# Small results in two halves of one PSUM bank, identity transposes spread over set-up and the last two sequences, and a new table of the order

## The chip, the core and the metric

The kernel runs on one core of a Trainium2 chip. Its time is the device time of one execution in microseconds (us). Each core has five engines that run their own instruction streams and meet by semaphores: PE (TensorE, matrix products), DVE (VectorE), ACT (ScalarE), POOL (GpSimd) and SP (SyncE, which here issues the DMAs). PE writes its results to PSUM, 8 banks of 128 partitions x 512 float32; DVE and ACT read them there. All other tiles are in SBUF.

## The reference

32 sequences of 256 tokens x 256 features, float32, go through two attention layers, each followed by a conditioned output block. What is computed, for one sequence:

```python
# layer 0: linear attention, 8 heads of 32
xn = ln(x, ln_w, ln_b)
q = softmax((xn @ Wq + bq) by head, over the 32 features)
k = softmax((xn @ Wk + bk + (1 - mask) * -1e6) by head, over the tokens)
v = (xn @ Wv + bv) * mask
y = q @ (k^T v)                       # per head
x = x + block(y, emb, ...)
# layer 1: full attention, 16 heads of 16
xn = ln(x, norm_w, norm_b)
q, k, v = xn @ q_w + q_b, xn @ k_w + k_b, (xn @ v_w + v_b) * mask
a = softmax(q k^T + (1 - mask) * -1e6)   # the mask goes by the key
y = a v
out = x + block(y, emb, ...)
# block
scale, shift = split(silu(emb) @ W_emb + b_emb)
block = silu(ln(y) * (1 + scale) + shift) @ W_out + b_out
```

Products are float32 in precision: each operand is split into a high and a low part, and three products of parts are added.

## The kernel before

Each sequence is cut into some 150 steps, each a small function that issues instructions on one engine: `scores` on PE, `maxima` on DVE, `exp` on ACT, and so on. Four parts of a sequence have letters that end the step's name in the tables: a is the input of layer 0 (load, normalisation, q, k, v, softmaxes, attention), b is the output block of layer 0, c is the input of layer 1 with its scores and weighted values, d is the output block of layer 1. Set-up (`prepared`) is a graph of the same kind: loads of the weights, folding of the norms into them (`w_sums`, `w_scaled`, `w_high`, `w_low`), the modulation (`e_product`, `e_sums`, `e_scaled`), the memsets of the score operands (`qk_zeros`, L510, two memsets of 128x2048 each, three times), and `identity`, `identity_r` (L269 to L275).

The order is written out in a table. STARTS gives each step of a sequence a planned start; sequence b's is PERIOD = 26.2851 later than that of b − 1. SHIFTS moves the parts a to d of the first three and last five sequences. SET_UP does the same for set-up. `in_order` (L113) sorts all steps by planned start and issues them in that order; a step whose tiles are not free waits in a list until they are. ROOM says how many tiles of each kind there are: 8 banks, for instance. Since one list decides, each engine's program order is fixed when the kernel is built, about five sequences being under way at once. On the chip, an engine runs its own list in order and stops where a semaphore is not yet there. These semaphores are put in by the framework from what each instruction reads and writes; in PSUM two engines are kept apart by the whole bank.

Layer 1 goes twice over the scores. First `scores` (L1029; two banks of 128x512) and `maxima` (L1041, DVE) find the maximum of each row. `max_high`, `max_low` (POOL) split it, `max_turn` (L1061, PE) turns it into rows, `max_row` (L1068, ACT) copies them out of PSUM, and a DMA (`max_place`) puts them into the operand of the second pass. There `scores` come again (L1096), `exp` (L1108, ACT), and `pv` (L1117, PE) weights the values: two for each half c of the features, v = 0 and 1, into one bank. `y_blocks` (L1136, DVE) transposes that bank, `y_sums` and `y_over` divide by the sums. `v_masked` (L1011, ACT) writes the operand va of pv, of which there are two buffers: it waits for the pv of two sequences before.

The output block of layer 1 (`normalized_blocks`, L621) takes statistics on DVE (`stats`, L625), adds them over partitions by a small product on PE (`means`, L630), goes on through `mean`, `spread` (DVE), `squared` (ACT), `added` (DVE), `variances` (PE, same bank), `variance` (DVE) to `deviation` (POOL), and then on to the gate and the product with W_out (`productd`, L558 like all split products). In layer 0, `attention` (L883, PE) writes a bank that `k_sums` and `blocks` (DVE) read.

The steps that the change touches took one of the 8 banks each: `means` with `variances`, `attention`, `max_turn`, and `pv` (one for v = 0 and 1). `warmed` (L277) is 16 transposes of the identity at the start of set-up, whose result nobody reads.

"Quick" sequences (the first EARLY = 2 and the last FINAL = 1) have some of POOL's work on DVE.

Of the kernel before, what the change touches and what calls it, by code (L numbers as in the profile page):

```python
# [10 lines left out]
F32 = mybir.dt.float32  # L11
# [12 lines left out]
    bank=8, xt=9, nrm=4, x=4, h=2, g=6, k0=3, ek=1, mk=1, q0=1, y=2, eqT=2, v0=2, att=1, qkp=1, qk=3,  # L24
# [7 lines left out]
NWARM = 16  # L32
# [4 lines left out]
    addedd=(120.61,), attentiona=(-13.38,), baseb=(-7.73,), based=(88.15,), blocksa=(-11.52,),  # L37
    centredd=(121.30,), deviationa=(-83.15,), deviationb=(-6.20,), deviationc=(24.49,), deviationd=(124.48,),
    dividedd=(125.42,), expc=(89.70, 92.11, 89.98, 91.28, 96.74, 97.83, 98.71, 99.15, 94.09, 94.56, 96.29,
    94.59, 101.15, 101.17, 101.20, 101.90), gateb=(-0.05,), gated=(129.02,), gatedb=(3.48,), gatedd=(133.75,),  # L40
    higha=(-72.32,), highc=(26.27,), k_expa=(-26.36,), k_kepta=(-19.92,), k_maxa=(-28.80,),
    k_producta=(-31.27,), k_sumsa=(-11.80,), k_turna=(-22.62,), loada=(-239.80,), lowa=(-51.26,), lowc=(29.93,),
    mask_rowa=(-53.49,), mask_rowsc=(33.40,), max_highc=(79.75,), max_lowc=(79.77,), max_placec=(88.54,),
    max_rowc=(82.68,), max_turnc=(82.00,), maximac=(55.40, 55.77, 56.53, 60.59, 56.43, 58.64, 64.05, 63.87,
    57.93, 60.08, 71.94, 73.05, 77.62, 78.88, 78.57, 77.29), meand=(116.76,), meansd=(116.59,),
    offseta=(-80.64,), offsetb=(-3.77,), offsetc=(24.78,), productb=(16.97,), productd=(142.80,), pvc=(92.35,
    100.35, 97.30, 103.38), q_expa=(-33.30,), q_lessa=(-33.32,), q_maxa=(-36.69,), q_producta=(-40.25,),
    q_turna=(-37.20,), q_turneda=(-11.84,), qk_highc=(33.74, 36.00), qk_lowc=(34.71, 41.81), qk_productc=(31.72,
    34.63), qk_wholec=(33.95, 40.07), resultb=(19.28,), resultd=(143.38,), scaleda=(-78.72,), scaledb=(-2.75,),
    scaledc=(25.24,), scoresc=(53.73, 56.51, 56.39, 60.97, 57.39, 70.48, 76.30, 75.27, 88.56, 89.96, 95.03,  # L50
    96.09, 92.06, 93.94, 99.31, 99.65), split_highb=(4.18,), split_highd=(135.42,), split_lowb=(13.04,),
    split_lowd=(138.42,), spreadd=(117.00,), squaredd=(119.35,), stack_lowc=(45.83,), stackc=(37.76,),
    statsa=(-103.45,), statsb=(-7.70,), statsc=(23.10,), statsd=(114.46,), stored=(150.83,), turna=(-73.69,),
    turnb=(-1.20,), turnc=(25.77,), turnedd=(128.51,), v_maskedc=(54.65,), v_productc=(51.60,),
    values_producta=(-24.01,), valuesa=(-22.73,), varianced=(122.21,), variancesd=(121.52,), wholea=(-72.30,),
    wholec=(28.29,), y_blocksd=(102.83, 105.24), y_overa=(-9.70, -8.79), y_overd=(104.23, 112.01),
    y_producta=(-10.85,), y_sumsa=(-9.72, -8.93), y_sumsd=(104.21, 108.21),
# [3 lines left out]
    0: (0.0, 0.0, 0.0, 0.0), 1: (0.0, 0.0, 0.0, 0.0), 2: (0.0, 0.0, 0.0, 0.0), 27: (0.0, 0.0, 0.0, 0.0),  # L61
    28: (0.0, 0.0, 0.0, 0.0), 29: (0.0, 0.0, 0.0, 0.0), 30: (0.0, 0.0, 0.0, 0.0), 31: (0.0, 0.0, 0.0, 0.0),
# [3 lines left out]
    bias_scaled=(-248.02,), cond_silu=(-161.41,), cond_tanh=(-332.90,), diag_made=(-816.08,), e_out=(-48.80,  # L66
    -2.85), e_product=(-96.24, -2.87), e_scaled=(-22.24, -1.46), e_sums=(-48.78, -2.83), identity=(-708.56,),
    identity_r=(-702.04,), load_bias=(-276.37,), load_bout=(-13.79, 53.66), load_cols=(-670.58,),
    load_cond=(-544.29,), load_emb=(-258.80, -217.52, -180.67, -207.44, -42.77, -14.95, -48.76, -2.89),
    load_masks=(-359.47,), load_w=(-291.77, -528.39, -390.22, -548.16, -39.72, -33.64, -88.51, -232.84),  # L70
    mask_terms=(-103.15,), p_made=(91.90, 5.63), qk_made=(-52.44, 60.07, 77.11), qk_zeros=(-61.21, -379.66,
    -674.55), qkp_made=(30.64,), terms0_store=(-141.84,), terms_rows=(-172.06,), terms_store=(-42.73,),
    terms_turn=(-333.70,), token_terms=(-574.41,), v0_made=(-369.51, -279.71), va_made=(-36.90, 52.97),
    w_high=(-50.10, -64.76, -198.98, -439.51, 25.73, 18.32, 14.13, -231.47), w_low=(-39.74, -58.97, -95.39,
    -307.80, 29.41, 24.14, 30.22, 4.56), w_rep=(-292.96, -366.10), w_scaled=(-76.66, -94.61, -210.46, 20.45,
    9.77, -47.81), w_sums=(-179.39, -114.53, -238.08, 19.55, 7.28, -54.52), warmed=(-409.56,),
    zero_one=(-762.96,), zero_one_store=(-98.07,),
# [87 lines left out]
def tile_two_layers(ctx: ExitStack, tc: tile.TileContext, a: dict, out: bass.AP):  # L165
# [34 lines left out]

    def f(ap):
        return ap.bitcast(F32)
# [49 lines left out]

    def prepared():
# [23 lines left out]
        def warmed():  # L277
            ps = bank()
            for n in range(NWARM):
                nc.tensor.transpose(ps[:, ts(n % 4, P)], ident, ident)  # L280

        o_cols = op("D", 0.3, load_cols)
        o = op("G", 0.9, identity)
        op("P", 0.11 * NWARM, warmed, o, take=("bank",), give=("bank",))
# [291 lines left out]
    def sequence(b):  # L576
# [44 lines left out]
        def normalized_blocks(*after):  # L621
# [8 lines left out]
            def means():  # L630
                s.m_sum = bank()
                nc.tensor.matmul(s.m_sum[:, 0:16], fold4, s.st[:, :, 1:6:3], start=True, stop=True)
# [21 lines left out]
            def variance():  # L654
                s.var = small.tile([P, NBLOCK], F32, name="var", bufs=4)
                nc.vector.tensor_reduce(s.var, s.m_sum[:, 16:32].rearrange("p (g n) -> p g n", n=2), AX.X, ALU.add)

# [21 lines left out]
            o = op("P", 0.15, means, o_s, take=("bank",))  # L679
# [5 lines left out]
            o = op("V", 0.12, variance, o, give=("bank",))  # L685
# [197 lines left out]
        def attention():  # L883
            s.a_ps = bank()[:, 0 : NC * 33].rearrange("p (c l) -> p c l", c=NC)
# [13 lines left out]
        def blocks():  # L898
            s.att = work.tile([P, NC, 4, 33], F32, name="att", bufs=ROOM["att"])
            for c in range(NC):  # L900
                nc.vector.scalar_tensor_tensor(
                    s.att[:, c], s.a_ps[:, c].unsqueeze(1).to_broadcast([P, 4, 33]), s.rk[:, c : c + 1], diag,
                    ALU.mult, ALU.mult,
                )

        o = op("P", 0.29, attention, o_k, o_v, take=("bank",), give=("k0", "v0"), mode=2)
        o = op("V", 0.12, k_sums, o)
        o_a = op("V", 0.42, blocks, o, done["diag"], take=("att",), give=("bank",))
# [152 lines left out]
        def max_turn():  # L1061
            s.m_ps = bank(F32R)
# [5 lines left out]
        def max_row():  # L1068
            s.m_row = work.tile([4 * NU * NC, S], F32R, name="m_row", bufs=ROOM["mrow"])
            nc.scalar.copy(s.m_row, f(s.m_ps[0 : 4 * NU * NC, 0:S]))  # L1070

# [5 lines left out]
        o = op("P", 0.13, max_turn, o, take=("bank",), give=("mx",))  # L1077
        o = op("A", 0.27, max_row, o, take=("mrow",), give=("bank",))
# [3 lines left out]
        s.yT_ps, s.yT = [None] * NC, [None] * NC  # L1082
# [5 lines left out]
        for c in range(NC):  # L1088
            o_pv = []
            for v in range(2):  # L1090
# [26 lines left out]
                def pv(c=c, v=v):  # L1117
                    if v == 0:
                        s.yT_ps[c] = bank()
# [118 lines left out]
```

## Time and profile before

| what | us |
|---|---|
| median of three runs (917.66, 918.82, 920.21) | 918.82 |
| the profiled execution | 914.85 |
| its span, from the first to the last instruction | 912.7 |
| PE busy | 864.9 |
| DVE busy | 813.5 |
| ACT busy | 700.2 |
| POOL busy | 692.4 |

The span is what the engines' records cover; 2.2 us of the execution lie around it. The profiled execution is 4.0 us under the median of the others. In the slices of the page each digit stands for 22.8 us: PE is at 9 tenths from the sixth to the thirty-eighth slice with no gap, lower in the head (6, 8, 7, 8, 8) and in the tail (7, 3). The line PEclk is the clock that was granted to PE: 6 and 7 tenths in the first two slices, 8 and 5 in the last two.

Of the groups, the longest on DVE are the maxima of the scores (324.9 us), on ACT the exponentials (270.2 us), on PE the split products of L558 (seven forms of some 80 to 150 us each).

### The profile page before, as it was taken

The page shows a single profiled execution, that of the slowest core. Times are in us where ns is not written, and L with a number is a line of the kernel's source. Part 1 is how long each engine was busy: PE and PEld are TensorE (multiplying, and loading weights), DVE is VectorE, ACT ScalarE, POOL GpSimd, SP SyncE. Part 2 cuts the span into 40 slices and gives each one's busy share as a digit, 9 for nine tenths or more (in the row PEclk, how much of TensorE's full clock was granted, in tenths as well). Part 3 has the DMA queues.
Part 4 walks back from the last instruction along what each step waited for, and adds up shares of the span by engine and source line. Part 5 has one row for each costly group of instructions (what it writes and reads, how often), then busy time and mean ns, then how long its engine had stood idle before and what let it go on. Part 6 is the DMA issues. An engine that isn't in the chain of part 4 may idle for free.

```text
span 912.7 us, 25210 instructions
## 1 busy us (share of the span) xinstructions
PE 864.9 (95%) x9494; PEld 705.0 (77%) x9494; DVE 813.5 (89%) x2235; ACT 700.2 (77%) x1420; POOL 692.4 (76%) x893
## 2 busy tenths in 40 slices
PE   6878899999999999999999999999999999999973
PEld 3667787888888888888888888888888888877642
DVE  6797989999999999999999999999999999999843
ACT  1365588788888898888888888888888888877762
POOL 5254567888888888988888888988888877775441
PEclk6799999999999999999999999999999999999985
DMA  6302222322232222223222212332233221222200
GB/s 215 108 16 88 84 81 81 102 104 97 103 103 74 89 71 90 102 104 103 96 104 86 86 60 92 104 102 104 96 104 103 71 82 57 87 86 86 95 14 24
DMA packets 56767, 81.09 MB, mean 89 GB/s; under 512 B 5407, under 2 KB 30021, under 8 KB 56646
## 3 DMA queue, kind: packets, MB, share of 16 engines
q1 hardware_dynamic: 56646, 79.47, 25.4%
q8 instruction: 76, 1.25, 0.6%
q14 instruction: 45, 0.37, 0.1%
HBM read 19.52 MB, written 8.55 MB: 31 GB/s over the span
## 4 chain that ended last, share of the span: by engine, by line
PE 79%; DVE 15%; POOL 2%; issue 1%; ACT 1%; DMA 0%; POOLq 0%; DVEq 0%; ACTq 0%
PE bank L558 37%; PE bank L1122 12%; PE bank L1100 9%; PE bank L1033 8%; PE bank L565 5%; DVE mx L1044 5%; PE bank L916 3%; PE bank L814 1%; PE bank L888 1%; DVE st L591 1%; PE bank L650 1%; PE bank L349 1%; DVE th L746 1%; DVE ident_r L270 1%; DVE yb L1138 1%
## 5 line engine op out<-in xcount | busy, mean ns | idle before, releaser
L1044 DVE TENSOR_REDUCE mx<-bank 128x2 f32<-128x512 f32 x512 | 324.9, 673 | 15.0 <-PE bank L1033 14.7
L1113 ACT ACTIVATE p<-bank 128x512 f32<-128x512 f32 x512 | 270.2, 600 | 84.1 <-PE bank L1100 78.5
L558 PE MATMUL bank<-xh,w_hi 128*128 128x256 f32 x512 | 153.1, 299 | 0.1
L558 PE MATMUL bank<-xl,w_hi 128*128 128x256 f32 x512 | 144.3, 282 | 1.2 <-DVE xl L707 1.2
L558 PE MATMUL bank<-xh,w_lo 128*128 128x256 f32 x512 | 143.9, 281 | 0.0
L1122 PE MATMUL bank<-p,va 128*32 128x256 f32 x2048 | 140.0, 386 | 0.1
L558 PE MATMUL bank<-wout_hi,hp 128*128 128x256 f32 x512 | 112.9, 302 | 10.0 <-ACT hp L752 9.5
L982 POOL TENSOR_TENSOR qk_lo<-nrm,qk_hi 128x512 fp32r<-128x512 f32 x58 | 74.7, 1287 | 56.5 <-ACT nrm L978 56.5
L1100 PE MATMUL bank<-qs,ks 64*128 64x256 f32 x1024 | 109.0, 311 | 4.3 <-DMA qs<-m_row 3.1
L1033 PE MATMUL bank<-ks,qs 64*128 64x256 f32 x1024 | 105.4, 307 | 1.0 <-DVE mx L1044 0.3
L1100 PEld LDWEIGHTS bank<-qs,ks 64*128 64x128 f32 x1024 | 73.8, 187 | 37.0 <-ACT p L1113 22.6
L558 PEld LDWEIGHTS bank<-xh,w_hi 128*128 128x128 f32 x512 | 97.1, 190 | 5.1 <-DVE mx L1044 0.4
L558 PEld LDWEIGHTS bank<-xl,w_hi 128*128 128x128 f32 x512 | 97.3, 190 | 1.6 <-DVE xl L707 1.6
L558 PEld LDWEIGHTS bank<-wout_hi,hp 128*128 128x128 f32 x512 | 86.3, 196 | 15.6 <-ACT hp L752 10.1
L1033 PEld LDWEIGHTS bank<-ks,qs 64*128 64x128 f32 x1024 | 73.6, 185 | 31.3 <-issue 13.4
L558 PEld LDWEIGHTS bank<-xh,w_lo 128*128 128x128 f32 x512 | 96.9, 189 | 0.0
L613 POOL TENSOR_SCALAR nrm<-xt,mv,off 128x256 f32<-128x256 f32 x116 | 65.0, 571 | 29.0 <-DVE off L608 26.1
L1122 PEld LDWEIGHTS bank<-p,va 128*32 128x32 f32 x2048 | 55.0, 109 | 41.1 <-ACT p L1113 1.8
L728 POOL TENSOR_TENSOR xt<-xt,bout 128x512 f32<-128x512 f32 x64 | 82.5, 1288 | 3.1 <-DMA bout<-in_bout_dram 3.1
L756 POOL TENSOR_TENSOR hp<-th,hp 128x512 fp32r<-128x512 f32 x58 | 74.9, 1292 | 9.1 <-ACT hp L752 9.1
L558 PE MATMUL bank<-w_hi,xh 128*128 128x256 f32 x256 | 78.2, 305 | 0.0
L707 POOL TENSOR_TENSOR xl<-nrm,xh 128x512 fp32r<-128x512 f32 x58 | 73.6, 1288 | 4.3 <-ACT nrm L703 4.3
(138 smaller groups left out, 2153.9 us busy)
## 6 DMA issues: line engine op xcount, KB each, us to landing
ks<-qk_hi SPq DMA_DIRECT2D x64, 256.0 KB
qs<-qk_hi SPq DMA_DIRECT2D x64, 256.0 KB
xt<-in_x_dram SPq DMA_DIRECT2D x32, 256.0 KB
ks<-qk_lo SPq DMA_DIRECT2D x32, 256.0 KB
qs<-qk_lo SPq DMA_DIRECT2D x32, 256.0 KB
out_dram<-xt SPq DMA_DIRECT2D x32, 256.0 KB
mk<-t_dram SPq DMA_DIRECT2D x32, 128.0 KB
raw<-in_w_dram SPq DMA_DIRECT2D x8, 256.0 KB
```

The lines of the kernel that those rows point to most:

```text
L558: nc.tensor.matmul(o, left, right, start=(n == 0), stop=(n == len(pairs) - 1))
L565: nc.tensor.transpose(ps[:, ds(c * S + t * P, P)], src[:, t, ts(c, P)], ident)
L613: (nc.vector if s.quick else nc.gpsimd).tensor_scalar(s.nrm[:, t, :], get()[:, t, :], s.mv[:, t, 1:2], s.off[:, t : t + 1], ALU.mult, ALU.add)
L707: engine.tensor_tensor(s.xp[1], s.whole, f(s.xp[0]), ALU.subtract)
L728: nc.gpsimd.tensor_tensor(s.x, s.x, bout[:, i : i + 1, :].to_broadcast([P, NT, D]), ALU.add)
L756: engine.tensor_tensor(s.hp[1], s.th, f(s.hp[0]), ALU.subtract)
L982: engine.tensor_tensor(s.qkp[1][:, :, c], s.qk_ps[c], f(s.qkp[0][:, :, c]), ALU.subtract)
L1033: nc.tensor.matmul(ps[w][:, ts(m, S)], s.qs[half(w), u, c, ts(m, P)], s.ks[half(w), u, c, :], start=True, stop=True,)
L1044: nc.vector.tensor_reduce(s.mx[:, :, w, u, c], halves(s.s_ps[0, c, u][w]), AX.X, ALU.max, negate=True)
L1100: nc.tensor.matmul(ps[w][:, ts(m, S)], s.ks[half(w), u, c, ts(m, P)], s.qs[half(w), u, c, :], start=True, stop=True,)
L1113: nc.scalar.activation(s.pt[c, u][:, w], s.s_ps[1, c, u][w], AF.Exp)
L1122: nc.tensor.matmul(s.yT_ps[c][32 * j : 32 * j + 32, ts(v, S)], s.va[:, m, 8 * c + 4 * v + j, :], s.pt[c, 2 * v + j // 2][:, j % 2, ts(m, S ...
```

## The change

- ROOM has 7 banks and 2 halves. One bank is a tile of its own, `halves_all`, of two halves of 256 columns. `means` with `variances`, `attention`, `max_turn` and `pv` take a half each instead of a bank. `pv` takes one for each v; `y_blocks` becomes two transposes of 128x256, one behind each pv; the second pv of a pair no longer depends on the first.
- `warmed` is a group of six transposes of the identity into a half. Set-up has 12 of them (72 transposes instead of 16), at planned starts from −1050 to 26. Each of the last two sequences has 12 more, which depend on its `max_place`.
- STARTS, SHIFTS and SET_UP have new values throughout; PERIOD is as it was. SHIFTS had only zeros.

What follows from the new tables for the order of the built kernel: in set-up, `zero_one` and all six memsets of `qk_zeros` stand together on POOL ahead of everything else but the identity (before: four memsets there, two after the first `deviation`); on SP the first load of x stands behind a load that waits for a `w_low`. In the loop, PE changes between tile shapes 17 times a sequence, 19 before. `y_blocks` of the second half of sequence n stands on DVE where it waits for `max_row` of n + 1 on ACT, in the same bank; `attention` on PE waits for that `max_row` as well, and `means` of n for DVE's `k_sums` of n + 5.

```diff
-    bank=8, xt=9, nrm=4, x=4, h=2, g=6, k0=3, ek=1, mk=1, q0=1, y=2, eqT=2, v0=2, att=1, qkp=1, qk=3,
+    bank=7, half=2, xt=9, nrm=4, x=4, h=2, g=6, k0=3, ek=1, mk=1, q0=1, y=2, eqT=2, v0=2, att=1, qkp=1, qk=3,
...
-NWARM = 16
+NWARM = 12
+NKEPT = 12
+LATEST = 2
...
+    halves_all = psum.tile([P, 2, 256], F32, tag="halves", name="halves", bufs=1)
+    halves_free = [0, 1]
+
+    def half_bank():
+        return halves_free.pop(0)
+
+    def in_half(n):
+        return halves_all[:, n]
...
+    def warmed():
+        n = half_bank()
+        for i in range(6):
+            nc.tensor.transpose(in_half(n)[:, ts(i % 2, P)], ident, ident)
+        halves_free.append(n)
...
-        def warmed():
-            ps = bank()
-            for n in range(NWARM):
-                nc.tensor.transpose(ps[:, ts(n % 4, P)], ident, ident)
...
-        op("P", 0.11 * NWARM, warmed, o, take=("bank",), give=("bank",))
+        for n in range(NWARM):
+            op("P", 0.66, warmed, o, take=("half",), give=("half",))
...
             def means():
-                s.m_sum = bank()
+                s.m_half = half_bank()
+                s.m_sum = in_half(s.m_half)
...
-            s.a_ps = bank()[:, 0 : NC * 33].rearrange("p (c l) -> p c l", c=NC)
+            s.a_half = half_bank()
+            s.a_ps = in_half(s.a_half)[:, 0 : NC * 33].rearrange("p (c l) -> p c l", c=NC)
...
         def max_turn():
-            s.m_ps = bank(F32R)
+            s.x_half = half_bank()
+            s.m_ps = in_half(s.x_half).bitcast(F32R)
...
                 def pv(c=c, v=v):
-                    if v == 0:
-                        s.yT_ps[c] = bank()
+                    s.yT_half[c, v] = half_bank()
+                    ps = in_half(s.yT_half[c, v])
...
-                o_pv.append(op("P", 0.904, pv, o_v, *o_pv, *exps, take=(() if v else ("bank",)), give=give, mode=2))
+                o_pv.append(op("P", 0.904, pv, o_v, *exps, take=("half",), give=give, mode=2))
...
-            def y_blocks(c=c):
-                s.yb[c] = work.tile([P, 2, NBLOCK, 32], F32, name="yb", bufs=ROOM["yb"])
-                nc.vector.transpose(s.yb[c].rearrange("p v g l -> p (v g l)"), s.yT_ps[c])
+            def y_blocks(c=c, v=0):
+                if s.yb[c] is None:
+                    s.yb[c] = work.tile([P, 2, NBLOCK, 32], F32, name="yb", bufs=ROOM["yb"])
+                nc.vector.transpose(s.yb[c][:, v].rearrange("p g l -> p (g l)"), in_half(s.yT_half[c, v]))
+                halves_free.append(s.yT_half[c, v])
...
+        if b >= B - LATEST:
+            for n in range(NKEPT):
+                op("P", 0.66, warmed, o_max, take=("half",), give=("half",))
```

The tables, cut to a few of their entries:

```diff
-    y_blocksd=(102.83, 105.24), ... max_rowc=(82.68,), v_maskedc=(54.65,), k_sumsa=(-11.80,), meansd=(116.59,),
+    y_blocksd=(104.74, 110.42, 113.74, 116.84), ... max_rowc=(90.11,), v_maskedc=(63.61,), k_sumsa=(-7.10,), meansd=(124.93,),
...
-    qk_zeros=(-61.21, -379.66, -674.55), warmed=(-409.56,),
+    qk_zeros=(-473.49, -765.87, -253.42), warmed=(-708.15, -305.26, -709.66, -166.17, -615.56, -208.90, -1050.40, 26.13, -118.92, -272.50, -280.34, -222.36),
```

## The prediction

> **What bounds the kernel now.** I read the engines' totals and the slices, then busy time by stretch, the chain inside one period, the waits, and the timelines of one period, the head and the tail.
>
> ```profile
> PE 864.9 (95%) x9494; PEld 705.0 (77%) x9494; DVE 813.5 (89%) x2235; ACT 700.2 (77%) x1420; POOL 692.4 (76%) x893
> PEclk6799999999999999999999999999999999999985
> ```
>
> ```profile
> 0.00:23.00 23.00, 15.38 (x44) 8.57 (x44) 15.78 (x42) 3.37 (x5) 12.65 (x18) 0.68 0.68 215
> 46.00:69.00 23.00, 17.86 (x161) 15.47 (x162) 22.19 (x68) 15.17 (x32) 13.18 (x18) 1.00 0.06 16
> 200.00:300.00 100.00, 100.00 (x1163) 82.78 (x1163) 92.86 (x257) 85.00 (x174) 88.47 (x115) 1.00 0.28 95
> 880.00:900.00 20.00, 14.58 (x119) 10.28 (x118) 8.10 (x27) 9.95 (x22) 6.34 (x7) 0.76 0.08 27
> ```
>
> Columns are length, busy PE, PEld, DVE, ACT, POOL, clock, DMA share, GB/s. From 200 to 300 us PE never stops, at full clock, with DVE at 92.86%. Head and tail leave PE open, at part of the clock. In the chain of that stretch:
>
> ```profile
> 234.95 2.81 PE bank L558 x24
> 260.40 2.81 PE bank L558 x24
> ```
>
> The same 24 products return after 25.45 us: one sequence. First scores of sequence 1 come at 105.42 and of sequence 27 at 767.40, so 26 periods of 25.46 us. What matters is whether PE stays without a wait. Cover for DVE is thin: 7% of 25.45 us is 1.8 us, of which 25.1/27 = 0.93 us is this wait for PE:
>
> ```profile
> DVE mean L636 <- PE bank L632: 25.1, 27, 5.2
> ```
>
> Durations that I use (groups; then ACT in one period):
>
> ```profile
> L1044 DVE TENSOR_REDUCE mx<-bank 128x2 f32<-128x512 f32 x512 | 324.9, 673 | 15.0 <-PE bank L1033 14.7
> L1138 DVE STREAM_TRANSPOSE yb<-bank 128x512 f32<-128x512 f32 x64 | 45.7, 714 | 0.8 <-PE bank L1122 0.7
> L628 DVE BATCH_NORM_STATS2 st<-y 128x6 f32<-128x64 f32 x256 | 35.1, 207 | 0.8 <-POOL y L1147 0.8
> ```
>
> ```profile
> 461.74 0.85 ACT L1014 ACTIVATE va<-bank,cols 128x256 f32<-128x256 f32 x2
> 462.45 0.87 ACT L840 ACTIVATE v<-bank,cols 128x256 f32<-128x256 f32 x2
> 463.16 0.34 ACT L1070 CAST m_row<-bank 32x256 fp32r<-32x256 f32 x1
> 464.45 0.57 ACT L818 COPY kk<-bank 128x512 f32<-128x512 f32 x1
> ```
>
> Head and tail (timelines):
>
> ```profile
> 1.81 7.11 DVE L270 CAST ident_r<-ident 128x128 fp32r<-128x128 f32 x1 [0.29 <-POOL ident masks.py:199]
> 7.02 1.82 POOL L510 MEMSET ks<- 128x2048 f32 x1
> 10.81 0.34 SPq L296 DMA_DIRECT2D raw<-in_w_dram  x1
> 11.70 1.21 PE L345 MATMUL bank<-bias,ident 6*128 6x256 f32 x2 [1.51 <-DVE bias L332]
> 878.19 1.23 PE L1100 MATMUL bank<-qs,ks 64*128 64x256 f32 x8 [3.12 <-DMA qs<-m_row]
> 896.30 0.44 PE L632 MATMUL bank<-st,fold 128*128 128x16 f32 x2
> ```
>
> A DVE cast of 128x128 takes 7.11 us there because POOL's first four memsets run until 8.84; DVE, then SP's fourth-weight load and PE's first sums, start behind it.
>
> **1. PE's own work per sequence.** The new order changes between full-height, half-height and narrow tiles 17 times a sequence instead of 19. Twelve L558 products take 1.43 us among their like and 1.61–1.63 next to other tiles, so one change costs about 0.19: −0.4 us. Matmuls are the same in number. PE alone would need 25.45 − 0.4 = 25.05 us. The second pv no longer waits for the first; both wait for ACT's exponentials, so I give that nothing.
>
> **2. The shared bank (decisive).** max_turn, means, attention and pv now write halves of one bank. In the program as built, waits between engines stand by the whole bank, although the halves are disjoint. So the DVE transpose y_blocks of sequence n waits for ACT's max_row of n+1, attention (PE) waits for max_row too, and means (PE) waits for DVE's k_sums of n+5, which had nothing to do with it. Queued behind y_blocks on DVE are maxima, statsd, q_turned and k_sums; queued behind means on PE is everything.
>
> I lay one period out from the first scores, with PE never waiting. The pv that frees the va buffer runs 0.67–1.67. ACT then needs va 0.84 (its row, two instructions), kk 0.52, m_row 0.33: with 0.04 us per hand-over (874.77 + 0.29 on PE, 875.10 on ACT) max_row ends at 3.4. DVE has run the three maxima ahead of y_blocks by 2.3 and waits 1.1. Then half a transpose 0.37 (half of 714 ns and a little), five maxima at 0.61 (six in 3.68 us back to back at 463.14) 3.06, reciprocal 0.16, statistics 1.01 (eight in 1.10), transpose of q 0.63, k_sums 0.15: 8.8. PE's means stands at 7.74. It waits 1.1 us; before, DVE waited for PE at this place.
>
> The loop: pv 1.00 + 0.84 + 0.52 + 0.33 + 0.37 + 3.06 + 0.16 + 1.01 + 0.63 + 0.15 + 0.14 for hand-overs = 8.21 us to means; from means to the next such pv PE has 25.05 − 7.07 = 17.98 us. Period 26.19, that is +0.74 × 26 = **+19 us**. Bounds: without the wait DVE reaches k_sums at 7.7, PE loses nothing and the period is 25.05 (−10 us); if ACT comes to va 0.6 us late (it is 85% busy, with gate, high, whole and v ahead of va) the period is 26.8 (+35 us). I take the sum, as its rows are of this very place.
>
> A rule against this change: the Trainium skill, "PSUM — Partial Sum Buffer", section "PSUM bank collisions raise a hardware error", wants engines kept apart by bank and quadrant, not by address. The build obeys that; no run here shows what overlapping would do. By addresses alone the sum would be the −10 us, by the rule the +19.
>
> **3. y_blocks split.** Two 256-wide transposes for one 512-wide, twice a sequence: about +0.14 us of DVE, between 0 and 2 × 0.2 (a reciprocal of 16 elements takes 0.23). It lies in the loop above only by its second half; the rest sits in DVE's spare time, and if that is gone it adds up to 0.14 × 26 = 4 us.
>
> **4. Head.** Six memsets now stand back to back on POOL, behind zero_one: 1.80 + 6 × 1.74 = 12.3 instead of 8.84, so identity_r ends 3.4 us later. From the cast to the first sums DVE took 2.74 us (8.96 to 11.70); a va_made (0.91 + 0.09) and the mask terms (17.41 to 18.44, 1.03) come into that stretch and a w_low (1.12) goes behind it: sums at 12.3 + 3.6 = 15.9 instead of 11.70. On SP the load of wout1 waits for that w_low (issued at about 17, not 10.81), and x of sequence 0 stands behind it and six more issues (0.3–0.6 us each): 20 instead of 5.14. On PE 72 transposes instead of 16: 24 of them run in early idle time, 42 stand between sums and e_sums, 42 × 0.213 = 8.9 us at half clock, 4.6 at full. First k_turn about 44 instead of 36.82. From 46 to 115 us PE is open (17.86–20.48 of 23), but DVE is at 22.19 of 23 from 46 to 69, so little is caught up; a clock held up from 30 on gives 1–2 back: **+6**, bounds +1 and +12.
>
> **5. Kept transposes in the last two sequences** (144). In the gap ahead of 878.19 three groups keep the clock, so productd of 29 (2.86 us at half clock) and the scores lose 1.4–2. Means of 31 no longer waits behind productd of 30 (2.6 us late at 896.30), but four groups stand ahead of it and two more ahead of varianced: 6 × 0.66 = 4, of which idle time hides 2. The last productd at full clock: −0.9 (3.24 us at half). Groups behind it cost nothing. Net **−1.5**, bounds −4 and, if the clock stays at half and a group takes 6 × 0.213 = 1.28, +4.
>
> Do transposes hold the clock? After the 16 set-up transposes, alone on PE, the granted clock is 1.00 from 4.95 to 8.36 us; it is 0.50 from 8.5 to 32. So they do. The Trainium skill, "TensorE: Matmul & The Clock Gate", Part 4, says full speed does not engage for transposes; this trace differs, and the measurement decides. By that rule the tail would be +2 and the head 4 us worse.
>
> **Sum.** +19 + 6 − 1.5 = +23.5 on the profiled 914.85 us (span 912.7 and 2.2 around it), 938.3. That run lies 4.0 under the median 918.82, so the median to expect is 942.
>
> **Rivals.** *(A) Other side: the bank's wait is hidden.* It decides at one point: max_row must end by about 2.4 us after the first scores, not 3.4, or the pv ahead of va must stand earlier in the real run. Then PE runs at 25.05: −10.4 + 6 − 1.5 = −6, 913. For it: before, va ran at 461.74, well ahead of kk. Against: the pv to wait for stands in PE's order just ahead. *(B) Half hidden:* period as before, +4.5: 923. For it: DVE's 0.93 us wait at mean is a cushion. *(C) ACT late or DVE the bound:* 26.8, 35 + 4.5: 958. For it: ACT's 78.5 us of waits for scores lie elsewhere in the period. Against: DVE's work is 23.8 of 26.8. *(D) The transposes do not hold the clock:* +6 on the forecast, 948; the row at 4.95 us speaks against it.
>
> **How the numbers follow.** Three runs spread over 2.5 us, so 0.3% (2.8 us) is about what can be told from none. Forecast 0.42 (932–950), A 0.23, B 0.17, C 0.10, D 0.08. Faster holds A and a little of B less its miss: 0.24; same 0.08, from the low end of B and the high end of A; slower 0.68. The range runs from just under A to C: 911 to 958.
>
> **What would show it.** Right: between 200 and 300 us PE below 97%, a wait of PE at the means (L650) or of DVE at the yb transpose for ACT's m_row, 1 us each about 26 times; first scores 26.2 us apart; first sums near 16 us, x of sequence 0 loaded from 20; clock 1.00 around 875–882. Wrong: PE at 100% with 25.0 us between first scores, or the head caught up by 105 us, or productd of 31 still at half clock.

## The result, and the profile after

The changed kernel takes 962.17 us (median of four runs, 957.98 to 964.37) against 918.24 us before: a ratio of 1.0475, 95% interval 1.0429 to 1.0522. The prediction had the sign, with 942 us, and missed the size: the time lies above its range of 911 to 958.

The profiled execution of the changed kernel took 963.03 us, 48.2 more than that of before; its span is 48.5 longer. The first scores of sequences 1 and 27 cut it into three parts:

| part | before | after | difference | predicted |
|---|---|---|---|---|
| start to first scores of sequence 1 | 105.4 | 111.1 | +5.7 | +6 |
| from there to those of sequence 27 | 662.0 | 699.1 | +37.1 | +19 |
| from there to the end | 145.3 | 151.0 | +5.7 | −1.5 |

The page of the changed kernel, engines and clock, and then its busy time from 200 to 300 us (PE is the first number with an x behind it, DVE the third, the clock is third from the end):

```profile
PE 887.0 (92%) x9694; PEld 729.7 (76%) x9694; DVE 838.5 (87%) x2299; ACT 705.7 (73%) x1420; POOL 692.8 (72%) x893
PEclk7899999999999999999999999999999999999989
```

```profile
200.00:300.00 100.00, 95.07 (x1074) 77.81 (x1072) 91.40 (x253) 80.86 (x163) 82.20 (x110) 1.00 0.24 85
```

PE, which had no gap in this stretch, is open for 4.9 us of 100, at full clock. First scores now return every 26.97 us (median of sequences 7 to 22), where they returned every 25.45. PE's gaps in one period of the changed kernel, from its timeline:

```profile
461.27 0.50 PE L1054 MATMUL bank<-ks,qs 64*128 64x256 f32 x3 [0.55 <-DVE th L765]
469.52 0.40 PE L650 MATMUL halves<-st,fold 128*128 128x16 f32 x2 [0.63 <-DVE rk L916]
```

The second line is the wait that was forecast: means (L650) stands until k_sums (L916) is through. The first was not: PE stands in the second pair of scores until DVE's gatedb (L765) gives the bank back. The time between starts of PE's instructions, set against the same instructions in run e13 below, where PE does not wait, gives all of it: 0.70 us ahead of means, 1.28 us at the first two pairs of scores; without these 2.0 us, PE's steps take 25.0 us, as was summed.

The chain that ended last, in the same period, cut to the pieces that matter:

```profile
461.27 0.50 PE bank L1054 x3
461.77 1.00 PE halves L1145 x16
...
463.87 0.37 ACT m_row L1092
464.24 0.02 issue
464.26 0.45 DVE yb L1162
...
469.41 0.07 DVE rk L916
469.48 0.04 issue
469.52 0.40 PE halves L650 x2
```

It goes from the scores through pv, max_row and the transpose to means, as laid out in the prediction, and from means over 7.9 us of PE to the end of productb (477.4). There DVE takes over: resultb starts at 477.47, and 10.6 us of DVE without a gap lead to the end of the next gatedb at 488.1 and to the scores behind it. It is one ring over PE, ACT and DVE, not a loop with a PE that runs free for 18 us.

What fills those 10.6 us shows in two pairs of rows, DVE's and POOL's of the same stretch:

```profile
478.68 0.76 DVE L625 SCALAR_TENSOR_TENSOR off<-mv 128x2 f32<-128x2 f32 x1
482.01 0.16 DVE L625 SCALAR_TENSOR_TENSOR off<-mv 128x2 f32<-128x2 f32 x1
485.17 0.79 DVE L625 SCALAR_TENSOR_TENSOR off<-mv 128x2 f32<-128x2 f32 x1
```

```profile
478.37 1.05 POOL L683 TENSOR_TENSOR y<-y,var 128x512 f32<-128x512 f32 x1
...
484.67 1.27 POOL L726 TENSOR_TENSOR xl<-nrm,xh 128x512 fp32r<-128x512 f32 x1
```

The instruction off (L625) multiplies minus the mean by the reciprocal deviation for each token of the normalisation; it works on 128x2 elements, and both its inputs are tensors in SBUF. It takes 0.16 us alone, and 0.76 or 0.79 where POOL's tensor-tensor instruction runs: 478.68 + 0.76 = 479.44 and 478.37 + 1.05 = 479.42; 485.96 and 485.94. DVE counts as busy all that time. It is so in the whole execution: 49 offs and 8 dd (L658, 128x16, also two tensors) began inside a POOL tensor-tensor of 128x512 with more than 0.3 us of it left. Each of the 57 took 0.7 us or more, and ended 0.02 to 0.03 us behind POOL's. The groups of the two kernels, 300 to 560 us (before, then after):

```profile
L608 DVE SCALAR_TENSOR_TENSOR off<-mv 128x2 f32<-128x2 f32 x32 | 4.4, 138 | 0.0
L640 DVE TENSOR_TENSOR dd<-st,mean 128x16 f32<-128x16 f32 x10 | 8.3, 830 | 0.3
```

```profile
L625 DVE SCALAR_TENSOR_TENSOR off<-mv 128x2 f32<-128x2 f32 x30 | 17.3, 578 | 0.0
L658 DVE TENSOR_TENSOR dd<-st,mean 128x16 f32<-128x16 f32 x10 | 2.9, 292 | 0.3
```

Three off per sequence cost 0.44 us more each. The kernel before had the same thing in another place: its dd, 128x16 elements, takes 0.83 us, and ends at 445.29 in the period looked at, where POOL's instruction ends at 445.25. There it cost the loop nothing: with dd rewritten (e17 below) the loop of that kernel stays as it is.

### The profile page after: what moved, and what is told of

It reads as the page before. It is cut to its first block, busy times and chain, and to the rows that moved or that the text cites. A ratio compares the mean times of both kernels' runs of the same rounds, so it can differ in the third digit from the quotient of the medians.

```text
span 961.2 us, 25684 instructions
## 1 busy us (share of the span) xinstructions
PE 887.0 (92%) x9694; PEld 729.7 (76%) x9694; DVE 838.5 (87%) x2299; ACT 705.7 (73%) x1420; POOL 692.8 (72%) x893
## 3 DMA queue, kind: packets, MB, share of 16 engines
q1 hardware_dynamic: 56646, 79.47, 23.8%
## 4 chain that ended last, share of the span: by engine, by line
PE 55%; DVE 37%; ACT 3%; issue 3%; POOL 1%; DMA 0%; POOLq 0%; DVEq 0%; ACTq 0%
PE bank L575 23%; DVE mx L1065 14%; PE halves L1145 11%; PE bank L1123 5%; PE bank L1054 4%; DVE st L645 3%; DVE yb L1162 3%; PE bank L582 2%; DVE th L765 2%; PE bank L937 2%; PE halves L271 2%; DVE eqT L892 2%; PE bank L833 2%; DVE ek L821 1%; PE halves L650 1%
## 5 line engine op out<-in xcount | busy, mean ns | idle before, releaser
L1065 DVE TENSOR_REDUCE mx<-bank 128x2 f32<-128x512 f32 x512 | 328.4, 668 | 1.7 <-PE bank L1054 1.7
L1145 PE MATMUL halves<-p,va 128*32 128x256 f32 x2048 | 137.5, 386 | 4.6 <-DVE var L674 3.5
L1054 PE MATMUL bank<-ks,qs 64*128 64x256 f32 x1024 | 126.9, 319 | 15.0 <-DVE th L765 12.0
L1054 PEld LDWEIGHTS bank<-ks,qs 64*128 64x128 f32 x1024 | 80.6, 185 | 54.8 <-DVE th L765 16.7
L575 PE MATMUL bank<-wout_hi,hp 128*128 128x256 f32 x512 | 107.6, 292 | 3.7 <-DVE hp L775 3.2
L1123 PE MATMUL bank<-qs,ks 64*128 64x256 f32 x1024 | 96.8, 298 | 2.9 <-DMA qs<-m_row 2.5
L575 PEld LDWEIGHTS bank<-wout_hi,hp 128*128 128x128 f32 x512 | 84.1, 190 | 16.2 <-ACT p L1136 10.5
L1162 DVE STREAM_TRANSPOSE yb<-halves 128x256 f32<-128x256 f32 x128 | 55.5, 433 | 45.5 <-ACT m_row L1092 29.8
L1145 PEld LDWEIGHTS halves<-p,va 128*32 128x32 f32 x2048 | 53.6, 109 | 44.4 <-DVE var L674 5.3
L885 POOL TENSOR_TENSOR eq<-eq,qmax 128x512 f32<-128x512 f32 x29 | 31.1, 1073 | 67.8 <-DVE qmax L881 67.8
```

The source lines that it names most:

```text
L575: nc.tensor.matmul(o, left, right, start=(n == 0), stop=(n == len(pairs) - 1))
L885: engine.tensor_tensor(s.eq, s.eq, s.qmax.unsqueeze(2).to_broadcast([P, NC * S // 32, 32]), ALU.subtract)
L1054: nc.tensor.matmul(ps[w][:, ts(m, S)], s.qs[half(w), u, c, ts(m, P)], s.ks[half(w), u, c, :], start=True, stop=True,)
L1065: nc.vector.tensor_reduce(s.mx[:, :, w, u, c], halves(s.s_ps[0, c, u][w]), AX.X, ALU.max, negate=True)
L1123: nc.tensor.matmul(ps[w][:, ts(m, S)], s.ks[half(w), u, c, ts(m, P)], s.qs[half(w), u, c, :], start=True, stop=True,)
L1145: nc.tensor.matmul(ps[32 * j : 32 * j + 32], s.va[:, m, 8 * c + 4 * v + j, :], s.pt[c, 2 * v + j // 2][:, j % 2, ts(m, S)], start=(m == 0) ...
```

## The experiments

e1, e2, e3, e5, e9 and e13 leave the order of the steps of the changed kernel as it is on every engine (but for the copy on ACT that e13 adds), and so does e6 but for the step that it leaves out; what they change is what an instruction waits for or how it is written. The others move or drop the steps that are named with them, and e7, e10 and e17 start from the kernel before. The column "us" is the one profiled execution, for e12, e15, e17 and e18 the median of 4, 4, 10 and 8 runs. The kernel before, run beside them, had medians from 914.7 to 919.3 and spread over 9 us in one sitting, so a few us between single runs tell nothing; the loop, from the trace, does. "Loop" is the median distance of first scores, sequences 7 to 22; the last columns are first scores of sequence 1, and first scores of sequence 27 to the end.

| run | us | loop | seq. 1 | 27 to end |
|---|---|---|---|---|
| before (profiled) | 914.85 | 25.45 | 105.4 | 145.3 |
| changed (profiled) | 963.03 | 26.97 | 111.1 | 151.0 |
| e1 max_turn in its own bank | 951.0 | 26.70 | 111.4 | 148.5 |
| e2 attention in its own bank | 952.7 | 26.68 | 110.6 | 147.9 |
| e3 both | 949.4 | 26.69 | 110.6 | 146.9 |
| e4 e1 and k_max behind gatedb | 946.1 | 26.54 | 109.8 | 148.4 |
| e5 off with one tensor operand | 932.9 | 25.69 | 107.6 | 149.9 |
| e6 e1 and no off | 1014.3 | 28.88 | 118.6 | 148.1 |
| e7 before, no off | 994.4 | 28.36 | 111.0 | 147.5 |
| e8 new table, whole banks | 943.2 | 26.36 | 111.6 | 147.8 |
| e9 e1 and e5 | 923.4 | 25.44 | 110.2 | 147.3 |
| e10 old table, halves | 1026.6 | 28.98 | 110.1 | 164.0 |
| e11 changed, old set-up | 976.5 | 26.97 | 126.0 | 148.5 |
| e12 e9, old set-up, none kept | 938.8 | 25.43 | 121.5 | 148.7 |
| e13 e9 and dd with one operand | 910.4 | 24.98 | 110.2 | 145.9 |
| e14 changed, a pair of memsets late | 957.6 | 26.99 | 107.0 | 149.4 |
| e15 e13 and e14 | 909.4 | 24.98 | 110.1 | 146.0 |
| e16 changed, none kept | 960.0 | 27.00 | 110.6 | 148.4 |
| e17 before, off and dd with one operand | 922.3 | 25.44 | 109.0 | 145.7 |
| e18 e8, off and dd with one operand | 925.2 | 25.49 | 112.0 | 149.5 |

### The shared bank: e1, e2, e3

```diff
 def max_turn():
-    s.x_half = half_bank()
-    s.m_ps = in_half(s.x_half).bitcast(F32R)
+    s.m_ps = bank(F32R)
...
 def attention():       # e2; e3 has both
-    s.a_half = half_bank()
-    s.a_ps = in_half(s.a_half)[:, 0 : NC * 33]...
+    s.a_ps = bank()[:, 0 : NC * 33]...
```

> The changed kernel, but max_turn writes a bank of the seven instead of a half; every engine's order is the same, only waits differ: the transpose y_blocks (DVE) no longer waits for max_row (ACT, 1.25 us of DVE idle per sequence in the changed kernel). Theory (ring): DVE and PE hold each other in one ring per sequence, resultb -> 10.6 us of DVE without a gap -> gatedb -> second scores -> pv -> va, kk, max_row -> y_blocks -> k_sums -> means -> productb -> resultb. Without max_row in it k_sums comes 1.25 us earlier, PE's wait at means (0.78) goes, its waits for gatedb at the scores (1.28) stay: period 26.97 -> 26.2 us, 963 -> about 943 us. Rival (DVE is simply full, the wait at the transpose is a wait that it would spend elsewhere): period stays above 26.7, time above 956. Second rival (the guard is all): 25.05, about 913.

> The changed kernel, but attention writes a bank of the seven instead of a half; same order on every engine. PE's means then waits for its own statistics instead of k_sums (0.78 us earlier), and attention no longer for max_row; DVE's y_blocks still waits for max_row. Ring theory: the two shared-bank waits lie in series in the same ring, so this alone also takes 0.7 to 0.8 us off: 26.2 us, about 943. Rival (DVE is full): above 26.7, above 956.

> Both edits together: only pv, means and variances share the bank; same order. Ring theory: the wait at means is taken away already by either edit, what stays is PE waiting for gatedb, 1.28 us: like either alone, 26.0 to 26.2 us, 938 to 943. If the waits add up instead: 25.05 to 25.4, 913 to 922.

The wait of the transpose for max_row is gone in e1, that of means for k_sums in e2, both in e3. All three give 26.7: a gain of 0.28 us a sequence, not the 0.77 or so expected. That either edit gives as much as both agrees with the ring; the size speaks for the rival, a DVE that is full. The groups of e1, 300 to 560 us, say with what:

```profile
L625 DVE SCALAR_TENSOR_TENSOR off<-mv 128x2 f32<-128x2 f32 x30 | 19.6, 653 | 0.2
L658 DVE TENSOR_TENSOR dd<-st,mean 128x16 f32<-128x16 f32 x10 | 8.4, 839 | 0.3
```

DVE idles 1.25 us less at the transpose, and stands 3 x 0.075 + 0.55 = 0.77 us longer in off and dd. Whoever comes earlier to an instruction that ends with POOL's has won nothing.

### k_max out of the queue: e4

```diff
-k_maxa=(-17.96,)
+k_maxa=(-16.90,)      # and max_turn as in e1; DVE's order changes at k_max alone
```

> max_turn in a bank of its own, and DVE's k_max (0.76 us) moved from ahead of gatedb to behind it; otherwise the same order. Ring theory: what is left in the ring is DVE's queue from resultb to gatedb, 10.6 us; with 0.76 less there PE's wait for gatedb falls from 1.28 to about 0.5: period about 25.4 to 25.5, about 922 to 926. Rival (DVE is full): as with max_turn's own bank alone.

0.15 us instead of 0.76. In e4 the first off after resultb starts at 469.13 and ends at 470.13, with POOL's instruction from 469.06 (1.05 us): it is POOL that sets when DVE goes on, and 0.76 us less of DVE's queue does not make POOL earlier. The expectation, a ring through DVE's queue alone, fell; so did a DVE that is full by its own work, in the next run.

### The instruction itself: e5

```diff
-nc.vector.scalar_tensor_tensor(s.off, s.mv[:, :, 0], -1.0, s.mv[:, :, 1], ALU.mult, ALU.mult)
+for t in range(NT):
+    nc.vector.tensor_scalar(s.off[:, t : t + 1], s.mv[:, t, 0:1], s.mv[:, t, 1:2], -1.0, ALU.mult, ALU.mult)
```

> The changed kernel with one DVE instruction written otherwise: off = -mean*rstd (128x2) takes two tensors from SBUF; it lasts 0.58 us on average here and 0.14 in the kernel before, and its long ones end within 0.02 us of the end of a POOL tensor-tensor instruction (479.44 against 479.42, 485.96 against 485.94). Here it is two instructions of 128x1 with the second operand as a per-partition scalar; same order on every engine. Theory (a DVE instruction with two SBUF tensors stands still while POOL's tensor-tensor runs): the two instructions take about 0.2 us together, DVE's stretch from resultb to gatedb is 0.9 us shorter, PE's wait for gatedb all but goes, the wait at means stays: period 26.97 -> about 26.1, 963 -> about 940 us. Rival (the 0.58 us are DVE's own pace or a wait for the semaphore of POOL's power): durations stay, two of them for one, time 963 to 985.

Two instructions in place of one, and 30 us less. 96 of them begin inside a POOL tensor-tensor of 128x512 with more than 0.3 us of it left; all take 0.18 to 0.22 us. The group and the waits of e5 that are left (300 to 560 and 300 to 600 us):

```profile
L626 DVE TENSOR_SCALAR off<-mv 128x1 f32<-128x1 f32 x60 | 9.8, 205 | 0.4 <-POOL mv L615 0.3
```

```profile
DVE yb L1165 <- ACT m_row L1095: 6.9, 11, 0.7
PE halves L653 <- DVE rk L919: 6.9, 11, 0.6
```

PE no longer waits for gatedb; the two waits by the shared bank stand. The loop falls by 1.28 us to 25.69, below the 26.1 expected; the wait of the transpose shrinks too (1.25 to 0.69 us at most), and what is left above PE's own 24.98 is the 0.7 us ahead of means. This is the largest single cause: from the first scores of sequence 1 to those of sequence 27 e5 takes 673.8 us where the changed kernel takes 699.1 and the kernel before 662.0, so 25 of the 37 us lost there. Of the rest of its 30 us, 3.5 lie in the head, where the clock differs as well (below), and 1 in the tail.

The Trainium skill, "SBUF — State Buffer", section "SBUF: two separate sides", says that DVE and GpSimd share a pair of ports as an exclusive lock, taken by a DVE instruction with two SBUF inputs against a GpSimd one that reads SBUF, and that the loser blocks until the other's instruction ends. The rows agree: ends within 0.04 us of each other, and no standing still with one tensor operand. One kind of row differs, and the measurement decides: POOL's power (0.70 us on 128x2, two tensors from SBUF) held none of the 24 offs that began inside it in the kernel before with more than 0.3 us of it left; they took 0.12 to 0.15 us.

### No off at all: e6, e7

```diff
-get()[:, t, :], s.mv[:, t, 1:2], s.off[:, t : t + 1], ALU.mult, ALU.add
+get()[:, t, :], s.mv[:, t, 0:1], s.mv[:, t, 1:2], ALU.subtract, ALU.mult
```

> max_turn in a bank of its own, and no off at all: the normalisation is (x - mean)*rstd instead of x*rstd + off. Same order otherwise. Theory (what holds the ring at 26.69 us in the run with max_turn's own bank is DVE, and 1.7 us of its stretch from resultb to gatedb are off standing still behind POOL): ring 25.0 us, so PE's own work decides: 25.05 to 25.2, 951 -> 910 to 914 us, level with the kernel before or a little under. Rival (DVE is full by itself, 24.7 of 26.7 us busy): only off's own 0.4 us, 26.3, about 941.

> The kernel before without off, as a control: PE has no wait there, so 3 x 0.14 us less on DVE per sequence change nothing in the loop: 913 to 917 us. If off's removal helps by itself (head, tail, or DVE after all the bound): below 910.

Both fell far wide, for a reason of their own, as the group of POOL in e7 shows (300 to 560 us):

```profile
L609 POOL TENSOR_SCALAR nrm<-xt,mv 128x256 f32<-128x256 f32 x40 | 48.5, 1221 | 1.0
```

The same instruction with mult and add takes 0.562 us in the kernel before, with subtract and mult 1.221. Six of them a sequence are 4 us more of POOL, which is then the bound (187 of 200 us busy). These runs say nothing on off; e17 is the control that e7 was meant to be.

### Table and code apart: e8, e10

e8 is the code of before with the new tables, e10 the code of the change with the old ones. e8 has the changed kernel's order on PE, ACT, POOL and SP but for the identity transposes; e10 has before's but for two places in the loop: one pv of each sequence stands three steps later on PE, and y_blocks is split. Set-up has 16 transposes in e8 and 18 in e10, and neither has the kept ones.

> The new table with the old tiles: 8 whole banks, y_blocks one transpose of 128x512 per pair of pv at the later of its two planned starts, 16 set-up transposes in one group, none kept; the order on every engine is that of the changed kernel but for these. No wait between unrelated small results. Theory (with the shared waits gone DVE's stretch with off held by POOL still decides): 26.5 to 26.7 in the loop, 943 to 952 us. Rival (the shared bank is the whole loss, the table is sound): 25.1 in the loop, 912 to 918.

> The kernel before with its old tables, but with the halves and the split pv and y_blocks of the change (y_blocks of both v at the old planned start; 18 set-up transposes, none kept). attention then waits for mean on DVE, pv for squared, varianced and y_blocks. Off stands where it stood, unheld (0.14 us). Theory (halves cost wherever the waits meet a PE that has no slack): 0.3 to 1.5 us a sequence, 923 to 955. Rival (the halves are harmless, the new table is the whole loss): 25.45 in the loop, 913 to 919.

e8 still has 26.36, with off at 0.525 us: without a shared bank, the new table is 0.9 us slower than the old one. And e10 has 28.98 with off at 0.139 us: with the old table, the halves and the moved pv, which were not tried apart, cost 3.5 us a sequence. Waits of e10, 300 to 600 us:

```profile
PE halves L1142 <- DVE yb L1159: 16.2, 22, 0.9
...
PE halves L1142 <- DVE att L918: 8.8, 10, 0.9
```

There pv waits for the transpose that empties the half before it, and for attention's blocks in the same bank. So the new table was needed for the halves, and most of what the halves could cost it avoids; what it did not avoid is that DVE stands behind POOL.

### Both causes away, then dd: e9, e13

```diff
 def mean():
-    s.mean = small.tile([P, NBLOCK], F32, name="mean", bufs=4)
-    nc.vector.tensor_reduce(s.mean, s.m_sum...)
+    s.mean_ps = s.m_sum[:, 48:56]
+    nc.vector.tensor_reduce(s.mean_ps, s.m_sum...)
 def spread():
-    ... s.mean.unsqueeze(2) ...
+    ... s.mean_ps.unsqueeze(2) ...
 def squared():
     ...
+    s.mean = small.tile([P, NBLOCK], F32, name="mean", bufs=4)
+    nc.scalar.copy(s.mean, s.mean_ps)      # POOL's centred now waits for squared, not for mean
```

> Both causes away: max_turn in a bank of its own and off as two instructions with one tensor operand each; same order on every engine as the changed kernel. Theory (DVE held by POOL, 1.28 us a sequence by the run with off rewritten, then the shared-bank waits of y_blocks and means, what is left of 25.69): PE without a wait, 25.05 to 25.25 in the loop, 933 -> 916 to 922 us. Rival (the bank is worth no more than the 0.28 us that it gave alone): 25.4, 925 to 927.

> The run with max_turn's own bank and off rewritten, and dd as well: mean goes to the shared half in PSUM, so that dd = st - mean has one tensor from SBUF; ACT copies mean to SBUF behind squared (0.19 us) for POOL's centring. Same order on every engine. In the run before this dd (128x16) took 0.97 us and ended with a POOL tensor-tensor instruction (451.70 against 451.66), and PE stopped for what DVE then had late (about 0.4 us a sequence). Theory (the same standing still): dd 0.15 to 0.3 us, loop 25.44 -> 25.05 to 25.15, total 923 -> 913 to 917 us. Rival (0.97 us is dd's wait for something else, or the PSUM operand makes it no faster): 25.4, 922 to 926.

e9 is e1 and e5 together; e13 adds the edit above. e9 stopped at 25.44, where its rival had it (25.4), though its time, 923.4, lies just under the rival's 925 to 927. The group of dd in e9 says why; PE's weight loads wait up to 0.4 us for what DVE then has late:

```profile
L661 DVE TENSOR_TENSOR dd<-st,mean 128x16 f32<-128x16 f32 x10 | 9.7, 968 | 0.3
```

With dd's second operand in PSUM, e13:

```profile
L661 DVE TENSOR_TENSOR dd<-st,halves 128x16 f32<-128x16 f32 x10 | 1.8, 175 | 0.3
```

```profile
300.00:500.00 200.00, 200.00 (x2364) 168.51 (x2352) 188.08 (x569) 172.82 (x362) 179.71 (x233) 1.00 0.27 94
```

dd falls from 0.97 to 0.175 us, PE has no gap from 300 to 500 us, and the loop is 24.98: PE's own work, for which the prediction had 25.05.

### Head and tail: e11, e12, e14, e16

e11 has the set-up table of before in the changed kernel; e14 moves one pair of memsets back; e16 drops the kept transposes; e12 is e9 with the old set-up and none kept.

```diff
-qk_zeros=(-473.49, -765.87, -253.42)      # e14
+qk_zeros=(-61.21, -765.87, -253.42)
-NKEPT = 12                                # e16
+NKEPT = 0
```

> The changed kernel with the set-up table of before (four memsets on POOL ahead, 18 set-up transposes in place of 72; loop and tail as changed). Theory (the head's 5.7 us at the first scores of sequence 1, 111.11 against 105.42, are the six memsets, the loads queued behind w_low and the transposes on PE): first sums back at about 11.7, first scores of sequence 1 at 105 to 107, total 957 to 959 us. Rival (the loop has slack to catch up, or the head's loss is from sequences 0 and 1 themselves): 962 to 964.

> Max_turn's own bank, off with one tensor operand, the set-up table of before, and no kept transposes in the last two sequences: what is left of the change is its order of the loop and the halves for the rest. Theory: loop 25.05 to 25.25 (-5 to -10 us against before), head as before, tail 2 us shorter than the changed kernel's for the groups behind the DMA of the row of maxima, 1 to 3 us longer for the clock at half: 908 to 916 us, faster than before by 0.3 to 1%. Rival (old set-up and new loop do not fit, or the tail needs the clock): 917 to 922.

> The changed kernel with the third pair of memsets of the score operands at its old planned start, behind the first sequences' deviation on POOL (with the DMAs that follow it); nothing else moved. Theory (DVE's rep and the cast of the identity stand still until POOL's memsets end, 12.3 us): they end at 8.9, first sums 16.74 -> 13.3, first q 38.8 -> 35.5 to 37, first scores of sequence 1 at 108 to 109.5 instead of 111.1; total 960 to 962. Rival (transposes or loads set the head): first q at 38 to 39, no change.

> The changed kernel without the 144 kept transposes of the last two sequences. Theory (three groups behind the DMA of the last row of maxima make the scores of sequence 31 start 2.2 us late, at 927.52 instead of 925.3; and without them the clock falls to half): scores 2 us earlier, the product with W_out of sequences 29 and 31 1.3 to 1.8 us longer each: first scores of sequence 27 to the end 149 to 152 us against 151.0, total 961 to 964. Rival (the transposes are the tail's loss): 146 to 148 us, 958 to 960.

e14 did what it should: first sums at 13.26 instead of 16.74, first scores of sequence 1 4.2 us earlier. But e15 has the same edit, its first sums at 13.26 too, and 110.1. The clock shows that the head is not one number. Its first stretch at half ends at 21.6 us in e14, 25.0 in e5, 27.0 in e15 and 30.4 in the changed kernel. Later it falls twice more in the changed kernel and not at all in e5, with the same order of steps (stretches 64:71 and 105:112, after and then e5):

```profile
64.00:71.00 7.00, 6.39 (x40) 6.00 (x39) 6.28 (x22) 2.74 (x6) 5.39 (x9) 0.76 0.00 0
105.00:112.00 7.00, 7.00 (x47) 6.42 (x46) 6.72 (x20) 3.98 (x8) 6.11 (x11) 0.76 0.01 2
```

```profile
64.00:71.00 7.00, 5.01 (x35) 4.06 (x35) 6.44 (x23) 6.36 (x14) 5.43 (x7) 1.00 0.07 20
105.00:112.00 7.00, 6.57 (x52) 5.43 (x52) 7.00 (x20) 6.23 (x15) 6.75 (x12) 1.00 0.01 2
```

In e5 sequence 1 starts its scores at 107.6, 2.2 us later than before, in the changed kernel 3.5 us after that. By estimate a dip to half for 3.4 us costs up to 1.7; how much of the 3.5 is the clock and how much off, which is faster in the head too, no run takes apart. The expectations of e11 and e12 were wrong: the old set-up in the new loop makes sequence 1 15 us later than in the changed kernel, and 11 later than in e9; e12 takes 1.024 of the kernel before (interval 1.0174 to 1.0308). In e11 the clock is 0.74 from 40 to 60 us and 0.61 from 60 to 80, where the changed kernel has 1.00 and 0.91. So the old set-up does not fit the new loop. The 54 transposes that it lacks do not explain the loss: e8 and e18 have the new set-up with 16 transposes instead of 72, and reach sequence 1 at 111.6 and 112.0. What in the old table does it was not taken apart.

In the tail, e16 is 2.6 us shorter than the changed kernel (148.4 against 151.0), between theory and rival: for all that they hold the clock (1.00 from 930 us to the end, where it is 0.50 from 940 on without them), the groups cost 2.6 us on balance. But e1, with all groups kept, has 148.5: with max_turn in its own bank, max_row no longer waits for pv (2.43 us of ACT's waiting at 922.20 in the changed kernel), so part of what the groups seem to cost lies in that wait. The totals of e14 and e16, 957.6 and 960.0, do not tell them from the changed kernel (957.98 to 964.37); only the traces do.

### The best version, and two controls: e15, e17, e18

> All of it: max_turn's own bank, off and dd with one tensor operand, the third pair of memsets late. Theory: loop 25.05 to 25.15, head 2 us shorter than the changed kernel's: 911 to 916, level with the kernel before or up to 0.7% faster. Rival (PE's own work is 25.44 as in the kernel before, what I summed from rows is wrong): 919 to 923.

> The kernel before with off and dd written with one tensor operand from SBUF, the control that the run without off could not be (POOL's normalisation took 1.22 us there instead of 0.57). In the kernel before, off is 0.14 us and dd 0.72 on average, and PE has no wait. Theory (PE alone bounds it): dd falls to about 0.2 us and nothing moves: 25.45 in the loop, 915 to 920, ratio 0.997 to 1.003. Rival (the gain of the run with all edits is DVE's, not the order's): 25.0, 905 to 910.

> The new table with 8 whole banks, no halves, the old 16 set-up transposes, none kept, off and dd with one tensor operand. Theory (the order of the loop is sound once DVE does not stand still; the halves bring nothing themselves): 24.98 in the loop as in the run with all edits; the head loses clock for want of transposes, 1 to 5 us: 908 to 916. Rival (the halves are needed, one bank more for the scores matters): 25.3 or more in the loop, 918 or more.

e15 takes 909.4 us (median of four) against 919.3 in the same sitting: 0.9896 of the kernel before, interval 0.9866 to 0.9927. That is 1% less than the kernel before, and 5% less than the changed one. e17 shows that the two rewritten instructions are not what gains: in the kernel before, the loop stays at 25.44, and the time is 1.0038 (1.0009 to 1.0067) of it, with several dips of the clock in the head of the profiled run. e18 shows that the halves, with the split transposes that go with them, do gain, against the expectation: with whole banks, whole transposes and the same order the loop is 25.49, 0.5 us more than e13. PE waits 0.28 us behind means for a bank; the rest is not located. (The head of e18 is at half clock until 42.8 us; its time is 1.0081 of the kernel before, interval 1.0056 to 1.0105.)

## Why the prediction was wrong, and where it was right

- **PE's own work, 25.05 us.** Right: 24.98 in e13, and 25.0 in the changed kernel without its waits. That fewer changes of tile shape make the difference was not tried by itself; by the shapes in the traces there are 21 a sequence before and 19 after, two fewer as was counted.
- **The shared bank as a loop of 8.21 us to means.** Mechanism right, 7.82 us measured from pv to means, PE's wait there 0.70 us for 1.1.
- **The step that failed: "from means to the next such pv PE has 25.05 − 7.07 = 17.98 us".** It took 19.15. PE waited again on the way, 1.28 us at the first scores, for DVE. The period was laid out "with PE never waiting" but at means, so DVE's queue from productb to gatedb had no term, and it was not spare: two offs stood still behind POOL there. Without that (e5) the loop is 25.69 instead of 26.97, and the middle part 25 us shorter. The kernel before had shown the same thing: its dd, 128x16, takes 716 ns on average, and the instruction that writes dd again, with one operand from PSUM, 138.
- **The bank, a period of 26.19 us where PE alone needs 25.05, so 1.14 us.** Mis-sized: e5, where off no longer holds DVE, has 25.69 where PE alone needs 24.98, 0.71 us. Undoing the waits gave only 0.28 as long as off held DVE (e1 to e3), and 0.25 with off away (e5 to e9), as dd then stood still in its place; only with dd free too (e13) is all of it gone. The price of the bank is not a number of its own: it depends on what holds DVE.
- **y_blocks split, +0.14.** 2 x 0.431 against 0.716 by the groups: +0.146 for a pair, which comes twice a sequence: 0.29, where 0.14 was put down for both.
- **Head, +6.** 5.7 measured, and the path to it as laid out: first sums at 16.74 (15.9), x of sequence 0 issued at 21.39 (20), first q and k_turn of sequence 0 at 38.80 and 44.70 (44 for k_turn). But the sum is right in part by luck: e5, with the same order, loses 2.2 us there, and the 3.5 between them go with the clock (at half until 30.4 us instead of 25.0, and two dips later) and with off. The sum had neither the dips nor off.
- **Tail, −1.5.** Wrong in sign: +5.7. 2.5 of it lies ahead of the first scores of sequence 31, 3.1 behind them. The clock held at the end, as forecast, but the groups cost 2.6 us on balance (e16): three of them stand in front of the last scores, where the sum had them hold the clock at no cost, and max_row waits 2.43 us for pv in the shared bank, which it did not have.
- **Rivals.** C had the right number for the loop, 26.8, "ACT late or DVE the bound", and was given 0.10. Its argument against, "DVE's work is 23.8 of 26.8", took DVE's durations from the kernel before, where off stood free. Neither ACT late nor a DVE full of its own work was the cause, so C's number is near by chance.

## What to carry to other kernels

A busy engine is not a working one: compare an instruction's duration with its size and with its own fastest instance, since one that stands still behind another engine's instruction shows as busy, not as a wait. When the order of the work moves, ask for each small DVE instruction with two SBUF tensors what POOL runs at that moment, and put one operand into PSUM or into a scalar where it can be held. And when a loop closes over several engines, a saving counts only if no instruction behind it in the loop ends when another engine's instruction ends.

## What the runs showed of the hardware

- DVE's off (two SBUF tensors, 128x2) took 0.12 to 0.16 us where no POOL instruction ran, and up to 1.24 in the changed kernel, ending with POOL's tensor-tensor of 128x512; with one tensor operand the two instructions took 0.18 to 0.22 us each (e5). Inside POOL's power on 128x2 (0.70 us, itself two tensors) it did not stand still in the kernel before: 0.15 us at 454.24, with POOL's from 454.23.
- POOL's tensor-scalar of 128x256 took 0.56 us with mult and add (before), 1.22 with subtract and mult (e7).
- Identity transposes held the granted clock: 1.00 from 930 us to the end in the changed kernel, 0.50 from 940 on without them (e16).
- The clock in the head fell to half for 3.4 us at 64 and at 105 us in the changed kernel, at neither in e5, which has the same order.
